# First attention of a two-layer decoder: eight heads to one context bank instead of four

## The chip, the cores and the metric

The kernel runs on one core of a Trainium2 chip. The metric is the device time of one execution in microseconds (us): the median of several runs. Beside it there is one execution recorded by the profiler, with every instruction's start and duration and every DMA packet.

Engines are named as in the profile: PE (TensorE, matrix products; PEld is its loading of weights, the stationary operand), DVE (VectorE), ACT (ScalarE), POOL (GpSimd), SP (SyncE, which issues DMAs here). A product's result lands in PSUM, which has eight banks of 128 partitions x 512 fp32; a quadrant is 32 of the partitions.

## The reference

Two layers on x of shape (8, 512, 256), each an attention and a feed-forward part, each with a residual. Only the first attention is touched by the change. With 16 heads of 16 columns, 8 batches and 512 tokens it computes

```
def _L0_attn_ref(hidden_states, attention_mask, rel_embeddings, Wq, bq, Wk, bk, Wv, bv, Wo, bo, ln_scale, ln_bias):
    ...
    scores = jnp.einsum('bhqd,bhkd->bhqk', q, k) / scale
    ...
    scores = scores + (c2p + p2c) / scale
    probs = jax.nn.softmax(scores, axis=-1)
    ctx = jnp.einsum('bhqk,bhkd->bhqd', probs, v)
    ctx = jnp.transpose(ctx, (0, 2, 1, 3)).reshape(B, S, H)
    out = ctx @ Wo + bo + hidden_states
    ...
```

c2p and p2c are scores of a query with embedded relative positions, and of a key with them. The result is normalized over its 256 columns and added to x. Everything is in fp32. After it come a feed-forward part with GELU, a second attention, and a mixture of 32 experts.

## The kernel before, in words

**Tiling.** `_l0_attention` (L90) walks over `steps` (L245): 8 batches b, 4 groups g of four heads (`NG`), 4 query tiles i of 128 tokens, 2 pairs p of heads. That makes 256 steps, 32 in a batch, 8 in a group. "Step 14" below is the step of that number within its batch; i and p follow from the number within the group (steps 0 and 1 have i = 0, steps 6 and 7 have i = 3; even steps have p = 0). The loop under `tc.manual_schedule()` (L478 to L532) is the order of the work: what a step issues goes to each engine's queue in the order written, so each engine works in order and waits at its first instruction whose data are not there.

**One step n** issues:
- `products` (L354): the scores of two heads, from `sm`, the projected queries and keys, into two PSUM banks `sc` (L363, K = 32). The pool of these banks has two, so the next step's products need the banks that DVE has read.
- `strips` (L298) for step n + 5 (`AHEAD`): position products (L306), copied by ACT (L313); a multiplication on POOL (L316); a DMA that writes them to memory in shifted rows (L323). The DMAs that read the windows `winp` and `winc` back (L332) and the two POOL additions (L343) follow one and two steps later.
- `near_keys` (L371): 4 or 6 transposes that add the windows into the score banks (L375). A step at i needs the window of i + 1, that is of step n + 2, as it landed.
- `weights` (L385): DVE adds `winc` and finds the row's extreme (L389); ACT takes the exponential and sums the row into `totals` (L391).
- `turned` (L394) for the step before: 8 PE instructions (an fp32 product is two) transpose the weights into a bank (L398), and DVE copies it out (L400).
- `weigh` (L403), on odd steps: the context of four heads for one query tile. Each head has 4 products (key tiles m) of v, 128 x 16 as weights, with `et`, 128 x 128 (L410). Head r writes rows 32 r to 32 r + 15 of the bank `ctx_ps`, one quadrant to a head, and leaves the other 16 rows of each quadrant at the zero of L237.
- one piece of side work: from `urgent`, or else from `side`, whose entries carry the step from which they may run (`later`, L252), and which is served strictly in order.

**Side work.** `project` (L275): queries and keys of the next group, two pieces at steps 0 and 1 of each group (L282). `values` (L267): v of the next batch, four pieces at steps 26 to 29 (L270, one DVE addition L273 each). `turn` and `normalized`: the next batch's normalized x, transposed. `divide`, `finish` and their parts:

When a group's last query tile is weighed (in the second step of the next group), ACT copies the bank (`c`, L421), DVE takes reciprocals of the totals (L424), and POOL spreads each of them over its head's 32 rows (`wide`, L426). `divide` (L439), queued three steps later, transposes `wide` on PE into `spread` (L442), and DVE multiplies (`cn`, L444). This happens for each of 4 groups. After the fourth group, `finish` (L447) queues four `out` (L452, one for each token tile): each sums, over the four groups' `cn`, products with `wo` (L455; `wo` has 32 rows for each head, 16 of them zero), DVE adds the result to xn (L458) and POOL adds the bias (L459). `measure` and `norm` (L461 to L469) finish the layer norm on DVE and POOL. For the last batch the four `out` are handed over as `rest` and run in `run` (L636) between the feed-forward part's first hidden products (L657).

In a batch the spreads run at steps 4 (last group of the batch before), 14, 22 and 30, and the `out` at steps 5, 6, 7 and 10.

**Start.** Outside the manual schedule, a scheduler orders the loads, the position keys (L172 to L207, with products on POOL, L203 and L206, that feed weight columns) and the clearing of eight `winc` tiles on POOL (L233).

Of the kernel before, what the change touches and what calls it, by code (L numbers as in the profile page):

```python
# [12 lines left out]
F32 = mybir.dt.float32  # L13
I32 = mybir.dt.int32
U32 = mybir.dt.uint32
AF = mybir.ActivationFunctionType
ALU = mybir.AluOpType
# [4 lines left out]
P = 128  # L22
B, S, H = 8, 512, 256
NT = S // P
NK = H // P
NH, HD = 16, 16
NG = 4
W = 256
WIN = 3 * P
NSHIFT = 4  # L30
# [59 lines left out]
def _l0_attention(nc, tc, a, x, ident, mhalf, carry, prefetch):  # L90
# [6 lines left out]
    with ExitStack() as ctx:  # L97
# [10 lines left out]
        wqk = carry.tile([P, 2, NK, NH, 32], F32, tag="w1", name="wqk")  # L108
        wq, wk = wqk[:, 0], wqk[:, 1]
        wv = wp.tile([P, NK, H], F32, tag="wv", name="wv")  # L110
        wo = carry.tile([P, NG, H], F32, tag="wo", name="wo")
        posw = carry.tile([P, 2, NG, W], F32, tag="w2", name="pos")
        posc, posp = posw[:, 0], posw[:, 1]
        bias = wp.tile([P, 4, NG], F32, tag="bias", name="bias")
# [3 lines left out]
        with tc.tile_pool(name="a_pos", bufs=1) as pp:  # L118
# [22 lines left out]
            for d in shift:  # L141
                nc.sync.dma_start(
                    d.rearrange("(q p) w -> p q w", p=P), zeros.unsqueeze(1).to_broadcast([P, 4, 2 * W])
                )
            nc.sync.dma_start(wo, a["wo_pad"].rearrange("(g p) m -> p g m", p=P))
            for name in ("bo", "ln_scale", "ln_bias"):
                nc.sync.dma_start(rows[name], a[name].partition_broadcast(P))
            for b in range(1, B):
# [76 lines left out]

        sb = pool("a_sb", 2)

        vs = [wp.tile([P, NT, H], F32, tag=f"v{n}", name=f"v{n}") for n in range(2)]

        winc = []  # L230
        for n in range(2 * NT):
# [2 lines left out]
            winc.append(w)  # L234

        ctx_ps = ps_c.tile([P, S], F32, tag="ctx", name="ctx_ps")
        nc.vector.memset(ctx_ps, 0.0)  # L237

        def near(i):

# [26 lines left out]
        def values(b, t):  # L267
            pv = misc("pv")
            for k in range(NK):
                nc.tensor.matmul(  # L270
                    pv[:, :H], xnT[:, k, t * P : (t + 1) * P], wv[:, k, :], start=k == 0, stop=k == NK - 1
                )
            nc.vector.tensor_tensor(vs[b % 2][:, t, :], pv[:, :H], rows["bv"], ALU.add)  # L273

        def project(b, g):  # L275

# [108 lines left out]
        def weights(n, j, sc):  # L385
            b, g, i, p = steps[n]
            e = sb.tile([P, S], F32, tag="e", name="e", bufs=4)
            low = sb.tile([P, 1], F32, tag="low", name="low", bufs=6)
            nc.vector.tensor_tensor_reduce(e, sc, wins[n][0][:, j, :], 1.0, -LOW, ALU.add, ALU.min, low)  # L389
            r = 2 * p + j  # L390
            nc.scalar.activation(e, e, AF.Exp, bias=low, scale=-1.0, accum_out=totals[b, g][:, i, r : r + 1])  # L391
            return e

        def turned(e):  # L394
# [8 lines left out]
        def weigh(n, ets):  # L403

            b, g, i, _ = steps[n]
            v = vs[b % 2]
            for m in range(NT):
                for r, et in enumerate(ets):
                    h = 4 * g + r
                    nc.tensor.matmul(  # L410
                        ctx_ps[32 * r : 32 * r + HD, i * P : (i + 1) * P],
                        v[:, m, HD * h : HD * h + HD],
                        et[:, m * P : (m + 1) * P],
                        start=m == 0,
                        stop=m == NT - 1,
                        skip_group_check=True,
                    )
            if i < NT - 1:
                return
            c = sb.tile([P, S], F32, tag="c", name="c", bufs=2)  # L420
            nc.scalar.copy(c, ctx_ps)  # L421

            rec = sb.tile([P, NT, 4], F32, tag="rec", name="rec")
            nc.vector.reciprocal(rec, totals.pop((b, g)))  # L424
            wide = sb.tile([P, NT, P], F32, tag="wide", name="wide", bufs=1)
            nc.gpsimd.tensor_copy(  # L426
                wide.rearrange("p i (r e) -> p i r e", e=32), rec.unsqueeze(3).to_broadcast([P, NT, 4, 32])
            )
            later(3, partial(divide, b, c, wide))
            if g == NG - 1:  # L430
                out, measure, norm = finish(b)
                if b == B - 1:
                    rest.extend([*[partial(out, t) for t in range(NT)], measure, norm])
                else:
                    later(3, *[partial(out, t, misc, sb) for t in range(NT)])
                    later(9, partial(measure, misc, sb))
                    later(12, partial(norm, misc, sb))

        def divide(b, c, wide):  # L439
            spread = ps_m.tile([P, S], F32, tag="misc", name="spread")  # L440
            for i in range(NT):
                nc.tensor.transpose(spread[:, i * P : (i + 1) * P], wide[:, i, :], ident)  # L442
            cn = carry.tile([P, S], F32, tag="cn", name="cn", bufs=5)
            nc.vector.tensor_tensor(cn, c, spread, ALU.mult)  # L444
            cns[b].append(cn)

        def finish(b):  # L447

            xn = xns[b % 2]
            stats = []  # L450

            def out(t, bank, pool):  # L452
                po = bank("po")
                for g in range(NG):
                    nc.tensor.matmul(  # L455
                        po[:, :H], cns[b][g][:, t * P : (t + 1) * P], wo[:, g, :], start=g == 0, stop=g == NG - 1
                    )
                nc.vector.tensor_tensor(xn[:, t, :], xn[:, t, :], po[:, :H], ALU.add)  # L458
                nc.gpsimd.tensor_tensor(xn[:, t, :], xn[:, t, :], rows["bo"], ALU.add)  # L459

            def measure(bank, pool):  # L461
                stats.extend(_batch_norm_stats(nc, pool, [xn[:, t, :] for t in range(NT)], 1e-7, mhalf))

            def norm(bank, pool):
                for t in range(NT):
                    _normalize(nc, xn[:, t, :], xn[:, t, :], *stats, t)
                    nc.gpsimd.tensor_tensor(xn[:, t, :], xn[:, t, :], rows["ln_scale"], ALU.mult)
                    nc.gpsimd.tensor_tensor(xn[:, t, :], xn[:, t, :], rows["ln_bias"], ALU.add)
                    nc.gpsimd.tensor_tensor(x[b][:, t, :], x[b][:, t, :], xn[:, t, :], ALU.add)  # L469

            return out, measure, norm
# [6 lines left out]
        with tc.manual_schedule():  # L478
# [7 lines left out]
            for now in range(len(steps) + 3):  # L486
                n = now
                if n < len(steps):
                    b, g, i, p = steps[n]
                    if (i, p) == (0, 0):  # L490
                        totals[b, g] = sb.tile([P, NT, 4], F32, tag="totals", name="totals", bufs=3)
                        if g in (0, NG - 1):
                            while side:
                                side.popleft()[1]()
                        if g + 1 < NG:
                            urgent.extend(project(b, g + 1))
                        elif b + 1 < B:
                            urgent.extend(project(b + 1, 0))
                            later(0, *[partial(values, b + 1, t) for t in range(NT)])
                        if g == NG - 2 and b + 1 < B:  # L500
                            measure, norm = normalized(sb, b + 1)
                            later(1, measure)
                            later(3, norm, *[partial(turn, b + 1, k) for k in range(NK)])
                    scs, parts = products(n)
                    parts.pop(0)()
                    more = parts.pop() if parts else None
                    if n + AHEAD < len(steps):
                        strips(n + AHEAD, more)
                    else:
                        if more is not None:  # L510
                            more()
                        for todo in (reads, adds):
                            if todo:
                                todo.pop(0)()
                    new = []
                    for j in range(2):
                        near_keys(n, j, scs[j])
                        new.append(weights(n, j, scs[j]))
                if n <= len(steps):
                    if es:  # L520
                        ets.extend(turned(e) for e in es)
                    es = new
                if n % 2 and len(ets) >= 4:
                    weigh(n - 3, [ets.popleft() for _ in range(4)])
                if urgent:
                    urgent.popleft()()
                elif side and side[0][0] <= n:
                    side.popleft()[1]()
                for f in prefetch.get(n - len(steps), ()):
                    f(misc, sb)  # L530
# [1073 lines left out]
    return out.reshape(*w.shape[:-1], NH * 32)  # L1604


def _experts(gate, up, down):

    first = np.concatenate([gate, up], axis=1).transpose(0, 2, 1).reshape(NE, NK, P, H).transpose(0, 2, 1, 3)
# [3 lines left out]
def _layout(v):  # L1613
# [1 line left out]
        "x": v["L0_attn_hidden_states"],  # L1615
        "wq_pad": _spread(v["L0_attn_Wq"]),
        "wk_pad": _spread(v["L0_attn_Wk"]),
        "wv": v["L0_attn_Wv"],
        "wo_pad": _spread(v["L0_attn_Wo"].T).T,
        "bq_pad": _spread(v["L0_attn_bq"]),  # L1620
        "bk_pad": _spread(v["L0_attn_bk"]),
        "bv": v["L0_attn_bv"],
        "bo": v["L0_attn_bo"],
        "ln_scale": v["L0_attn_ln_scale"],
        "ln_bias": v["L0_attn_ln_bias"],
# [35 lines left out]
```

## Time and profile before

| what | us |
| --- | --- |
| median of 3 runs | 2162.43 |
| lowest, highest run | 2162.23, 2166.1 |
| the profiled execution | 2158.92 |
| its span, first to last instruction | 2157.1 |
| first attention within it, to | about 1152 |

The profile's page gives busy time for each engine, then 40 slices of 53.9 us with the busy share in tenths. PEclk is the granted clock of TensorE in tenths of full speed. DMA is the mean busy share of 16 DMA engines. Groups of instructions are named by line and engine, with "result <- operands", shape and count, then busy time and the mean duration of one in ns, then idle time of that engine just before them. Overlapping instructions count once as busy; four products on four quadrants overlap, so their group's busy time is less than count times duration. PE durations are modelled and contain a latency, so what a stretch of PE work costs is read from its start to the start of what follows. In the order of time, a line has start, time covered, engine, line, operation, names, shapes and count, and in brackets how long the engine sat idle before and who released it.

The groups in the attention that the change is about, over the whole run: L410 has 4096 products of 274 ns and as many loads; L455 256 products of 389 ns; L442 128 of 273 ns; L421 32 copies with a median of 562 ns on ACT; L424 32 of 243 ns and L444 32 of 677 ns on DVE; L426 32 of 610 ns on POOL; L273 32 of 424 ns on DVE.

### The profile page before, as it was taken

The numbers are of one execution on the slowest core, as the hardware profiler recorded it, in microseconds if no ns is written. First come the engines' busy times: TensorE is split into PE (matmuls) and PEld (weight loads), VectorE is DVE, ScalarE is ACT, GpSimd is POOL, SyncE is SP. The second block draws the span as 40 slices with busy tenths as digits, with TensorE's granted clock in tenths as the row PEclk, the third lists the DMA queues.
The fourth block names the chain that finished last, engine by engine and source line by source line (L and its number), as shares of the span: only waits on it lengthen the run. The fifth ranks groups of instructions, "written<-read, shape, count | busy, mean of one in ns | idle before, by whom it ended". The sixth has DMA issues, their size and how long they took to land.

```text
span 2157.1 us, 46358 instructions
## 1 busy us (share of the span) xinstructions
PE 1989.8 (92%) x16100; PEld 1439.5 (67%) x16100; DVE 1401.4 (65%) x3716; ACT 1112.0 (52%) x2382; POOL 1140.5 (53%) x1342
## 2 busy tenths in 40 slices
PE   7999999999999999999998999989988877499997
PEld 4777777777777777767775666645554445388886
DVE  2576676766767677676776655337887776356666
ACT  2776666676666767667662211244444423144443
POOL 4666766767667667676673210112544544355555
PEclk7999999999999999999999999999999987699999
DMA  8998888898898988889893344900111113656888
GB/s 271 317 295 274 273 277 275 277 291 259 265 284 256 296 265 278 281 266 291 266 303 107 100 148 140 122 18 11 46 41 39 51 44 112 248 164 204 260 261 266
DMA packets 389175, 444.50 MB, mean 206 GB/s; under 512 B 43345, under 2 KB 368209, under 8 KB 388945
## 3 DMA queue, kind: packets, MB, share of 16 engines
q1 hardware_dynamic: 374160, 402.20, 61.7%
q0 software_dynamic: 13824, 38.29, 4.8%
q8 instruction: 132, 2.16, 0.4%
q10 hardware_dynamic: 960, 1.05, 0.2%
q14 instruction: 99, 0.80, 0.1%
HBM read 239.26 MB, written 202.19 MB: 205 GB/s over the span
## 4 chain that ended last, share of the span: by engine, by line
PE 27%; DVE 10%; issue 4%; POOL 4%; DMA 3%; ACT 2%; POOLq 0%; DVEq 0%; ACTq 0%; SPq 0%
PE po L665 5%; PE pge L1421 4%; PE ph L657 3%; POOL results L860 2%; PE poe L1439 2%; PE pq L916 2%; PE ao L1006 1%; DVE prod L777 1%; PE po L1035 1%; PE pv L928 1%; DVE value L777 1%; PE ps L953 1%; DVE st L52 1%; DVE xn L62 1%; PE ptr L1413 1%
## 5 line engine op out<-in xcount | busy, mean ns | idle before, releaser
L389 DVE CUSTOM_DVE_ANT_0 e<-sc,winc 128x512 f32<-128x512 f32 x512 | 333.3, 688 | 294.9 <-PE sc L375 133.6
L391 ACT ACTIVATE e<-e,low 128x512 f32<-128x512 f32 x512 | 365.9, 716 | 111.2 <-DVE low L389 105.9
L313 ACT COPY strip<-pa 128x512 f32<-128x512 f32 x512 | 275.3, 591 | 212.7 <-issue 81.3
L316 POOL TENSOR_TENSOR own<-aside,strip 128x512 f32<-128x512 f32 x256 | 268.5, 1049 | 217.5 <-ACT strip L313 198.7
L363 PE MATMUL sc<-sm,sm 32*128 32x256 f32 (+3 forms) x1792 | 323.0, 440 | 15.4 <-DVE low L389 15.4
L400 DVE COPY et<-et_ps 128x512 f32<-128x512 f32 x512 | 328.5, 683 | 0.3 <-PE et_ps L398 0.2
L306 PE MATMUL pa<-pos,sm 32*128 32x256 f32 x2048 | 301.6, 408 | 2.3 <-ACT strip L313 1.3
L398 PE MATMUL et_ps<-ident,e 128*128 128x128 f32 x2048 | 266.4, 273 | 0.2 <-DVE et L400 0.2
L860 POOL DMA_INDIRECT rows<-pay,slot x128 | 141.6, 1106 | 229.5 <-issue 216.3
L363 PEld LDWEIGHTS sc<-sm,sm 32*128 32x128 f32 x1792 | 162.3, 184 | 124.6 <-issue 49.6
L398 PEld LDWEIGHTS et_ps<-ident,e 128*128 128x128 f32 x2048 | 232.6, 142 | 0.6 <-ACT e L391 0.5
L343 POOL TENSOR_TENSOR winp<-winp,own 128x256 f32<-128x256 f32 x256 | 186.5, 728 | 74.8 <-DMA winp<-shift 63.7
L860 POOL DMA_INDIRECT results<-y,r x160 | 155.8, 974 | 122.1 <-ACT y L1441 74.7
L375 PE MATMUL sc<-ident,winp 128*128 128x128 f32 x1280 | 199.7, 285 | 5.3 <-DMA winp<-shift 5.0
L343 POOL TENSOR_TENSOR winc<-winc,own 128x256 f32<-128x256 f32 x256 | 186.6, 729 | 34.1 <-DMA winc<-shift 31.0
L306 PEld LDWEIGHTS pa<-pos,sm 32*128 32x128 f32 x2048 | 180.9, 188 | 15.0 <-ACT strip L313 4.7
L375 PEld LDWEIGHTS sc<-ident,winp 128*128 128x128 f32 x1280 | 136.3, 141 | 81.4 <-issue 63.2
L57 POOL TENSOR_TENSOR rstd<-var,mhalf 128x4 f32<-128x4 f32 x40 | 44.8, 1121 | 252.6 <-DVE var L55 230.6
L1421 PE MATMUL pge<-store,rT 128*128 x640 | 167.9, 385 | 1.1 <-DVE rT L1415 0.5
L410 PE MATMUL ctx_ps<-et,v 128*16 128x128 f32 x4096 | 137.2, 274 | 0.2 <-DVE et L400 0.2
L660 ACT ACTIVATE hT<-ph,b 128x512 f32<-128x512 f32 x64 | 44.0, 687 | 169.8 <-PE ph L657 169.8
L282 PE MATMUL pq<-xnT,wqk 128*128 128x512 f32 x256 | 126.1, 614 | 3.6 <-DVE xnT L77 3.6
(216 smaller groups left out, 3421.4 us busy)
## 6 DMA issues: line engine op xcount, KB each, us to landing
shift<-strip SPq DMA_DIRECT2D x256, 510.0 KB
winp<-shift SPq DMA_DIRECT2D x128, 384.0 KB
winc<-shift SPq DMA_DIRECT2D x128, 384.0 KB
winp<-shift SPq DMA_DIRECT2D x128, 256.0 KB
winc<-shift SPq DMA_DIRECT2D x128, 256.0 KB
rows<-empty SPq DMA_DIRECT2D x8, 2640.0 KB
r<-rows SPq DMA_DIRECT2D x160, 132.0 KB
z<-results SPq DMA_DIRECT2D x32, 512.0 KB
```

The source lines that it names most:

```text
L306: nc.tensor.matmul(pa[:, t * W : (t + 1) * W], src[rs, i * P : (i + 1) * P], pos[rs, g, :], start=True, stop=True)
L313: nc.scalar.copy(st[:, 2 * j : 2 * j + 2, :].rearrange("p t w -> p (t w)"), pas[j])
L316: nc.gpsimd.tensor_tensor(own, aside.unsqueeze(2).to_broadcast([P, 2, 2, P]), st[:, :, W - 1 : W].rearrange("p (j t) o -> p t j o", t=2).t ...
L343: nc.gpsimd.tensor_tensor(dst, dst, own[:, t], ALU.add)
L363: nc.tensor.matmul(sc[:, c0:c1], s[side_][rs, cut : cut + P], s[2 + side_][rs, c0:c1], start=c0 == 0, stop=False, skip_group_check=True,)
L375: nc.tensor.matmul(sc[:, m * P : (m + 1) * P], wins[n + 2 * (m - i)][1][:, j, (i - m + 1) * P : (i - m + 2) * P], ident, start=False, stop ...
L389: nc.vector.tensor_tensor_reduce(e, sc, wins[n][0][:, j, :], 1.0, -LOW, ALU.add, ALU.min, low)
L391: nc.scalar.activation(e, e, AF.Exp, bias=low, scale=-1.0, accum_out=totals[b, g][:, i, r : r + 1])
L398: nc.tensor.transpose(et_ps[:, ms], e[:, ms], ident)
L400: nc.vector.tensor_copy(et, et_ps)
L860: ins = nc.gpsimd.indirect_dma_start(to, bass.IndirectOffsetOnAxis(ap=index, axis=0), source, None, bounds_check=last)
L1421: nc.tensor.matmul(pg[:, :H], rT[:, k * P : (k + 1) * P], w[:, k * H : (k + 1) * H], start=k == 0, stop=k == NK - 1)
```

## The change

Two groups, 2 k and 2 k + 1, share the context bank. In each quadrant the even group's head has the first 16 rows and the odd group's the last 16. For this, v is kept as 32 columns for each head, 16 of them zero: in the first half for heads of even groups, in the second for heads of odd ones, so that a product of 32 columns adds zeros to the other head's rows. The two halves of v are cleared once, on POOL, and written by two DVE additions for each token tile. Only the first product on each quadrant, of the even group at i = 0, starts a new sum in the bank. `wv` and `bv` come with their columns in the order even groups, odd groups. `totals` holds eight heads. The copy of the bank, the reciprocals, `wide` and `divide` run once for two groups, after the odd one; `out` sums over two `cn` instead of four, and `wo` has 256 rows without zeros. The number of context products, 16 for each weigh (32 PE instructions), stays. In a batch, the spreads of steps 14 and 30 no longer occur.

```diff
+NC = NG // 2
@@
-        wo = carry.tile([P, NG, H], F32, tag="wo", name="wo")
+        wo = carry.tile([P, NC, H], F32, tag="wo", name="wo")
@@
-            nc.sync.dma_start(wo, a["wo_pad"].rearrange("(g p) m -> p g m", p=P))
+            nc.sync.dma_start(wo, a["wo_rows"].rearrange("(g p) m -> p g m", p=P))
@@
-        vs = [wp.tile([P, NT, H], F32, tag=f"v{n}", name=f"v{n}") for n in range(2)]
+        vs = [wp.tile([P, NT, 2, NH // 2, 2 * HD], F32, tag=f"v{n}", name=f"v{n}") for n in range(2)]
+        for v in vs:
+            nc.gpsimd.memset(v, 0.0)
@@
-        nc.vector.memset(ctx_ps, 0.0)
@@
-            nc.vector.tensor_tensor(vs[b % 2][:, t, :], pv[:, :H], rows["bv"], ALU.add)
+            by_head = lambda w: w.rearrange("p (h d) -> p h d", d=HD)
+            for o in range(2):
+                s = slice(o * H // 2, (o + 1) * H // 2)
+                nc.vector.tensor_tensor(
+                    vs[b % 2][:, t, o, :, HD * o : HD * o + HD], by_head(pv[:, s]), by_head(rows["bv"][:, s]), ALU.add
+                )
@@
-            nc.scalar.activation(e, e, AF.Exp, bias=low, scale=-1.0, accum_out=totals[b, g][:, i, r : r + 1])
+            r = 2 * r + g % 2
+            nc.scalar.activation(e, e, AF.Exp, bias=low, scale=-1.0, accum_out=totals[b, g // 2][:, i, r : r + 1])
@@
-                        ctx_ps[32 * r : 32 * r + HD, i * P : (i + 1) * P],
-                        v[:, m, HD * h : HD * h + HD],
+                        ctx_ps[32 * r : 32 * r + 32, i * P : (i + 1) * P],
+                        vs[b % 2][:, m, g % 2, g // 2 * 4 + r, :],
                         et[:, m * P : (m + 1) * P],
-                        start=m == 0,
-                        stop=m == NT - 1,
+                        start=m == 0 and i == 0 and not odd,
+                        stop=m == NT - 1 and odd,
@@
-            if i < NT - 1:
+            if i < NT - 1 or not odd:
                 return
@@
-            rec = sb.tile([P, NT, 4], F32, tag="rec", name="rec")
-            nc.vector.reciprocal(rec, totals.pop((b, g)))
+            rec = sb.tile([P, NT, 8], F32, tag="rec", name="rec")
+            nc.vector.reciprocal(rec, totals.pop((b, g // 2)))
@@
-                wide.rearrange("p i (r e) -> p i r e", e=32), rec.unsqueeze(3).to_broadcast([P, NT, 4, 32])
+                wide.rearrange("p i (r e) -> p i r e", e=HD), rec.unsqueeze(3).to_broadcast([P, NT, 8, HD])
@@
-                for g in range(NG):
+                for g in range(NC):
                     nc.tensor.matmul(
-                        po[:, :H], cns[b][g][:, t * P : (t + 1) * P], wo[:, g, :], start=g == 0, stop=g == NG - 1
+                        po[:, :H], cns[b][g][:, t * P : (t + 1) * P], wo[:, g, :], start=g == 0, stop=g == NC - 1
                     )
@@
-        "wv": v["L0_attn_Wv"],
-        "wo_pad": _spread(v["L0_attn_Wo"].T).T,
+        "wv": _odd_last(v["L0_attn_Wv"]),
+        "wo_rows": v["L0_attn_Wo"].reshape(NC, 2, 4, HD, H).transpose(0, 2, 1, 3, 4).reshape(H, H),
```

## The prediction

> **What bounds the kernel now.** I read the page first, then stretches of the first attention, the groups by line and shape, and the order of time inside single steps.
>
> ```profile
> span 2157.1 us, 46358 instructions
> PE 1989.8 (92%) x16100; PEld 1439.5 (67%) x16100; DVE 1401.4 (65%) x3716; ACT 1112.0 (52%) x2382; POOL 1140.5 (53%) x1342
> PE   7999999999999999999998999989988877499997
> PEclk7999999999999999999999999999999987699999
> DMA  8998888898898988889893344900111113656888
> ```
>
> The change lies in slices 1 to 21 (the first attention, to about 1152 us). TensorE is at nine tenths there with its full clock, and the DMA engines are at eight to nine tenths: two candidates. A stretch of about one batch (32 steps; the same spread starts at 248.70 and again at 386.26, so 137.6 us), columns length, PE, PEld, DVE, ACT, POOL, clock, DMA share, GB/s:
>
> ```profile
> 200.00:340.00 140.00, 136.59 (x1567) 102.72 (x1565) 98.78 (x241) 95.94 (x218) 96.09 (x121) 1.00 0.89 278
> ```
>
> PE is busy for 97.6%. DVE, ACT and POOL have 30% to spare; DMA has 11%. What PE waits for shows inside it: I took each stretch of equal matmuls and the time to the next stretch, and compared it with the shortest of its kind. Of the 1092 us from 60 to 1152, 78 are above those shortest times; most recur in each batch where a score bank is released late by VectorE (0.47 to 0.61 us in a step in which PE has nothing beside it), not by a DMA. So PE's own work is some 93% of this stage, and work taken out shortens it wherever no such wait takes its place.
>
> **Projection.** `out` issues for each token tile 4 fp32 products over K=128, as 8 PE instructions (two passes); the change leaves 2 products, 4 instructions. What an `out` of 4 costs is in the profile already: `values` has the same form (128*128, 128x256, x4), in the same place of a step and with one VectorE add behind it. Two answers in order of time, an `out` and a `values`, both behind the context products:
>
> ```profile
> 346.17 1.99 PE L455 MATMUL po<-wo,cn 128*128 128x256 f32 x8
> 348.09 0.59 PE L363 MATMUL sc<-sm,sm 32*128 32x384 f32 x2
> ```
>
> ```profile
> 443.24 1.13 PE L270 MATMUL pv<-wv,xnT 128*128 128x256 f32 x4
> 444.31 0.48 PE L363 MATMUL sc<-sm,sm 32*128 32x256 f32 x2
> ```
>
> From start to next start: 348.09 - 346.17 = 1.92 us against 444.31 - 443.24 = 1.07; the difference, 0.86, is four instructions at 0.215 (256 rows, two passes). 28 outs run in the attention (7 batches x 4): 28 x 0.86 = 24.1 us. The last batch's 4 run between the first hidden products of the FFN, where PE runs without a gap from 1160 to 1184: another 4 x 0.86 = 3.4. Does the shorter step stay PE-bound? The steps with `values` take 3.62 and 4.81 us (even, odd), against 4.48 and 5.68 with `out`: they keep the difference, under the same VectorE load. Projection: -27.5 us.
>
> **Softmax division.** It goes from 32 to 16 runs. Removed 16 times: ACT's copy c (0.562 us), DVE's product cn (0.677), POOL's wide (0.610), 4 PE transposes; 32 reciprocals of 0.243 become 16 of 128x32 (estimate 0.26, from 16 more elements in each). That is 9.0 us of ACT, 14.4 of DVE and 9.8 of POOL, none of them the bound. On PE a spread is worth little, since it fills a wait:
>
> ```profile
> 386.26 0.60 PE L442 MATMUL spread<-ident,wide 128*128 128x128 f32 x4
> 387.62 1.20 PE L363 MATMUL sc<-sm,sm 32*128 32x384 f32 x3 [0.76 <-DVE low L389]
> ```
>
> ```profile
> 455.18 0.60 PE L442 MATMUL spread<-ident,wide 128*128 128x128 f32 x4
> 455.71 0.74 PE L363 MATMUL sc<-sm,sm 32*128 32x384 f32 x2
> ```
>
> In each batch four spreads run, at steps 4, 14, 22 and 30. The changed schedule drops those of steps 14 and 30 (groups 0 and 2). The first of these two rows is step 14: the score products wait 0.76 us longer for VectorE, which normalizes the batch before it. Without the spread they wait until the same moment: gain 0. The second is step 30 (3.12 us). Without the spread PE's own work is 0.49 + 0.97 + 1.08 = 2.53, but a step with nothing beside it waits about 0.47 us for VectorE: 3.00. Gain 0.12 x 8 = 1.0 us. The bounds: 0, and, if all waits went too, 16 x 0.44 + 8 x 0.83 = 13.6 us (a spread is worth 0.87 + 0.53 - 0.97 = 0.44 on a PE without waits). I take 1.0, which the two rows support.
>
> **Context products, now 32 columns wide.** Their number stays 4096, but each loads 128x32 weights instead of 128x16, half of them zeros.
>
> ```profile
> L410 PEld LDWEIGHTS ctx_ps<-et,v x4096: 92/97/97, 71.9 to 1151.4; 128*16 128x16 f32 x196
> ```
>
> ```profile
> L953 PEld LDWEIGHTS ps<-prod,heads x192: 106/109/178, 1431.7 to 1785.3; 128*32 128x32 f32 x192
> ```
>
> The wide load takes 12 ns more. Where does it land? The products run as rounds of four, one for each quadrant; the rounds start 109 ns apart (in one weigh at 606.913, 607.022, 607.131 us), which is also the spacing of the L398 transposes (8 in 0.87 us), whose 128-column loads take 142 ns. A load eight times as wide thus hides behind a stream of 128 rows, and so will this. Only the first round of a weigh has nothing to hide behind: 128 x 0.012 = 1.5 us. Here a rule speaks against the change: the Trainium skill, "TensorE: Matmul & The Clock Gate", Part 3 (The mechanism, "What overlaps and what doesn't") lets a weight load overlap running matmuls only if the row groups differ. All these loads use all rows. By the rule every load is exposed, 4096 x 0.012 = 49 us more; by the row 1.5. If it held, the L398 stream couldn't keep 109 ns a piece; I take the row, and keep the rule as a rival.
>
> **The rest.** `values` writes v in two VectorE adds of 128x128: 2 x 0.288 (the row of L1427, same size, from a bank) for 0.424, so 0.15 us in each of 32 places; VectorE is idle 0.78 us before the next score in such a step. Cost 0; 32 x 0.15 = 4.9 if that cover is gone, and not below 0. The totals' column stride changes no count. PE accumulates even and odd groups in one bank, so the only wait for its copy now comes after two groups: gain 0 to 1. At the start POOL clears two v of 128x2048 (twice a winc memset of 0.95 each, 3.6 us pipelined) ahead of the weight products L203; today three winc memsets and 1.53 us of idle time stand there (4.25 us), so it fits. The winc memsets move behind, some 4 us later, to about 30 us; the first window read goes out at 45. Cost 0, at most 3. On SP the order is the same; wo's load halves (256 KB less, about 0.9 us at 274 GB/s), and nobody waits for it then: 0. VectorE's memset of the context bank ran while it waited for x: 0.
>
> **DMA.** The steps shorten by 3.4 us a batch and the DMA work stays: share 0.89 x 137.6 / 134.1 (137.6 - 4 x 0.86) = 0.91, while 60 to 200 us ran at 0.95. Counting packets by size in a batch, a window read lands about 4 us after issue and is used 1 to 4.7 us later. The reads whose two steps contain outs have 2.1 to 4.3, and lose at most 1.7. I book 1 us given back; between 0 and, if half of the projection's gain in the attention goes into waits, 12.
>
> **Sum** against the profiled execution (2158.92 us; 2157.1 and 1.8 around the span): -27.5 - 1.0 + 1.5 + 1.0 = -26.0, so 2132.9. The median of the runs before, 2162.43, lies 3.5 above that execution; I carry the difference over: 2136.4, given as 2136.
>
> **Rivals.**
> 1. Waits for windows take over (up to 12 us more than booked): 2137 to 2149. For: 0.91 to 0.95 is near the highest share seen, and DVE e waited 31.6 us in all for winp. Against: PE waited 5 us for windows in the whole stage, and the spare times above. 0.13.
> 2. The removed division takes its waits along: 2136 less up to 12.6, so 2124. For: the 0.83 wait behind the spread recurs in most batches. Against: VectorE's normalization causes it and stays. 0.09.
> 3. Slower: loads in the context products are exposed, 12 ns in each. 2136 + 47.5 = 2184. It decides from 26 us on, which is 6.5 ns a load. Against: 109 ns a round leaves nothing exposed today. 0.03.
> 4. It does not do what it says, that is, outs don't shorten their steps, since VectorE or the windows set them: about 2162. Against: `values` steps. 0.03.
> Forecast: 2129 to 2143, 0.72.
>
> The range for 8 in 10 is 2126 to 2148: all of the forecast, most of rival 1, part of 2. A difference under 0.2% (4.3 us) can't be told from none. Faster 0.94 (forecast, 1, 2), same 0.03 (4), slower 0.03 (3).
>
> **What would show it.** Right: `po` with 128 PE instructions, 1.06 us to the next score products behind context products; even and odd steps with an out near 3.6 and 4.8; rounds of context products still 109 ns apart with loads of about 109 ns; a batch of 134 us; step 30 at 3.0 and step 14 unchanged. Wrong: rounds at 120 ns or more (rival 3); PE `sc` L375's successor waiting for `winp` in steps 5 to 12, with a DMA share at 0.95 (rival 1); step 14 shorter by 0.8 (rival 2). The second attention and the experts should not move; if they do, the cause is not in this sum.

## The result, and the profile after

| | before | changed |
| --- | --- | --- |
| median of 4 runs, us | 2162.73 | 2134.41 |
| lowest, highest, us | 2162.23, 2166.1 | 2132.01, 2136.61 |
| the profiled execution, us | 2158.92 | 2132.52 |
| one batch (32 steps, median of batches 1 to 6), us | 137.5 | 134.4 |

The ratio is 0.9862 with a 95% interval of 0.9846 to 0.9879. The predicted 2136 is 1.6 us above the median, and inside the runs.

The page of the changed kernel, with the rows that answer to those shown of before:

```profile
span 2130.7 us, 46004 instructions
PE 1963.5 (92%) x15908; PEld 1415.5 (66%) x15908; DVE 1393.8 (65%) x3715; ACT 1104.7 (52%) x2366; POOL 1138.3 (53%) x1328
PEclk7999999999999999999999999999999987699999
DMA  8998989898898989989883544900111114556788
```

PE lost 192 instructions (128 of the outs, 64 of the spreads), 26.3 us of its busy time and 26.4 us of the span: work on the engine that is the bound came out, and its share of the span stayed at 92%. The same stretch of 140 us as before, same columns:

```profile
200.00:340.00 140.00, 136.80 (x1581) 102.54 (x1580) 100.44 (x248) 98.02 (x223) 98.30 (x123) 1.00 0.92 286
```

PE is as busy as it was (136.80 us against 136.59), but more steps fit: DVE, ACT and POOL do more in it, and the DMA share is 0.92 instead of 0.89. Two steps with an `out`, PE in order of time; the first is behind context products, as the two rows in the prediction were:

```profile
476.88 1.13 PE L463 MATMUL po<-wo,cn 128*128 128x256 f32 x4
477.94 0.59 PE L371 MATMUL sc<-sm,sm 32*128 32x384 f32 x2
...
480.38 1.03 PE L463 MATMUL po<-wo,cn 128*128 128x256 f32 x4
481.34 0.59 PE L371 MATMUL sc<-sm,sm 32*128 32x384 f32 x2
```

477.94 - 476.88 = 1.06 us to the next score products, where it was 1.92. Measured from one step's near-key products (L383) to the next's, the four steps of a batch with an `out` went from 5.68, 4.27, 5.46 and 4.48 us to 4.83, 3.40, 4.61 and 3.62: 0.85 to 0.87 each. Steps 14 and 30, which lost their spread, stayed as they were (4.40 and 4.39 us, 3.12 and 3.12). The context products, by their own row (min/median/max in ns):

```profile
L418 PEld LDWEIGHTS ctx_ps<-et,v x4096: 106/110/178, 70.8 to 1123.8; 128*32 128x32 f32 x196
```

The load of 32 columns takes 13 ns more than that of 16 (median 97 before). From the second on, the rounds of four that it belongs to still start 109 ns apart; only the time from the first to the second round of a weigh grew, from 0.120 us (606.793 to 606.913 before) to 0.134 (610.097 to 610.231 now).

### The profile page after: what moved, and what is told of

It is laid out like the page before. It is cut to its first block, busy times and chain, and to the rows that moved or that the text cites. A ratio compares the mean times of both kernels' runs of the same rounds, so it can differ in the third digit from the quotient of the medians.

```text
span 2130.7 us, 46004 instructions
## 1 busy us (share of the span) xinstructions
PE 1963.5 (92%) x15908; PEld 1415.5 (66%) x15908; DVE 1393.8 (65%) x3715; ACT 1104.7 (52%) x2366; POOL 1138.3 (53%) x1328
## 4 chain that ended last, share of the span: by engine, by line
PE 32%; DVE 10%; issue 4%; ACT 2%; SPq 1%; DMA 1%; POOL 1%; POOLq 0%; DVEq 0%; ACTq 0%
PE pge L1430 7%; PE po L674 5%; PE poe L1448 3%; PE ph L666 3%; PE pq L925 2%; PE ao L1015 2%; PE ptr L1422 2%; DVE prod L786 1%; PE pv L937 1%; DVE value L786 1%; PE po L1044 1%; SPq L1387 1%; PE ps L962 1%; DVE st L53 1%; DVE xn L63 1%
## 5 line engine op out<-in xcount | busy, mean ns | idle before, releaser
L351 POOL TENSOR_TENSOR winp<-winp,own 128x256 f32<-128x256 f32 x256 | 186.9, 730 | 76.8 <-DMA winp<-shift 63.0
L383 PE MATMUL sc<-ident,winp 128*128 128x128 f32 x1280 | 199.6, 285 | 5.8 <-DMA winp<-shift 5.8
L383 PEld LDWEIGHTS sc<-ident,winp 128*128 128x128 f32 x1280 | 136.4, 141 | 80.7 <-issue 59.6
L418 PE MATMUL ctx_ps<-et,v 128*32 128x128 f32 x4096 | 140.0, 277 | 0.2 <-DVE et L409 0.2
```

The costliest lines, as they stand in the source:

```text
L351: nc.gpsimd.tensor_tensor(dst, dst, own[:, t], ALU.add)
L383: nc.tensor.matmul(sc[:, m * P : (m + 1) * P], wins[n + 2 * (m - i)][1][:, j, (i - m + 1) * P : (i - m + 2) * P], ident, start=False, stop ...
```

## The experiments

The medians of the kernel before were 2166.05, 2172.2 and 2177.49 us on the three chips used here, so ratios to it are compared, not times. The expectations are in the times of the first chip; a ratio times 2162.73 puts a result on that scale. "Changed" is the kernel after the change. Lines of the edits that are left out are marked "...".

**e1: the projection's two products put back.** `wo` of the changed kernel gets two more slabs, cleared to zero on POOL, and each `out` four products again; the sums stay the same.

```diff
-        wo = carry.tile([P, NC, H], F32, tag="wo", name="wo")
+        wo = carry.tile([P, NG, H], F32, tag="wo", name="wo")
...
+            nc.gpsimd.memset(wo[:, NC:, :], 0.0)
...
-                for g in range(NC):
+                for g in range(NG):
...
-                        po[:, :H], cns[b][g][:, t * P : (t + 1) * P], wo[:, g, :], start=g == 0, stop=g == NC - 1
+                        po[:, :H], cns[b][g % NC][:, t * P : (t + 1) * P], wo[:, g, :], start=g == 0, stop=g == NG - 1
```

> The changed kernel, but each out issues 8 PE instructions again: two more products, with a wo of zeros, are summed into the same bank. Nothing else moves; the division stays at 16 runs. Theory (the gain is the projection's PE time): 28 outs in the attention and 4 in the FFN get 0.86 us back each, +27.5: about 2162 us (2157 to 2166), with steps 5, 6, 7 and 10 at 5.69, 4.26, 5.46 and 4.48 us again. Rival (the halved division carries a part of the gain): the time stays well below the kernel before, 2140 to 2152.

Measured: 2161.19 us, ratio 0.998 (0.997 to 0.999). PE in order of time, in step 6 of the batch shown above:

```profile
489.21 1.89 PE L464 MATMUL po<-wo,cn 128*128 128x256 f32 x8
491.03 0.59 PE L372 MATMUL sc<-sm,sm 32*128 32x384 f32 x2
```

1.82 us to the next score products, against 0.96 in the changed kernel. The four steps are back at 5.69, 4.27, 5.47 and 4.48 us and a batch at 137.5. With the projection's products back, 0.2% (0.1 to 0.3) is left of the change's 1.4%: the gain is the projection. What the 0.2% is stays open; no step of the attention accounts for it.

**e2: the division put back.** After each even group the changed kernel also copies the bank, takes reciprocals, spreads and multiplies; the result is not used.

```diff
-            if i < NT - 1 or not odd:
+            if i < NT - 1:
                 return
+            if not odd:
+                ...
+                nc.scalar.copy(c, ctx_ps)
+                ...
+                nc.vector.reciprocal(rec, totals[b, g // 2][:, :, 0::2])
+                ...
+                later(3, partial(divide, b, c, wide, False))
```

> The changed kernel, with a division after each even group as well (copy of the bank, reciprocals, wide, 4 transposes, multiplication), at its old places in steps 14 and 30; its result is not used. Theory (the spreads of steps 14 and 30 only fill waits for VectorE): steps 14 and 30 stay at 4.39 and 3.12 us, total 2134 to 2138. Rival (the division takes its waits along): 0.44 to 1.3 us for each of 16, so 2141 to 2155.

Measured: 2140.34 us, ratio 0.9878 (0.9861 to 0.9895), on the scale of the first chip 2136.3, as the theory had it; the interval overlaps that of the changed kernel. The steps decide: 14 and 30 take 4.38 and 3.12 us with the spread and 4.39 and 3.12 without, and batches 1 to 6 take 805.1 us together against 806.6 in the changed kernel. PE in step 30 of a batch, first in this kernel, then in the changed one:

```profile
581.98 1.04 PE L407 MATMUL et_ps<-ident,e 128*128 128x128 f32 x8
582.86 0.60 PE L461 MATMUL spread<-ident,wide 128*128 128x128 f32 x4
583.38 0.74 PE L371 MATMUL sc<-sm,sm 32*128 32x384 f32 x2
...
584.61 0.66 PE L383 MATMUL sc<-ident,winp 128*128 128x128 f32 x4
```

```profile
581.77 1.04 PE L407 MATMUL et_ps<-ident,e 128*128 128x128 f32 x8
582.74 1.17 PE L371 MATMUL sc<-sm,sm 32*128 32x384 f32 x3
...
584.40 0.66 PE L383 MATMUL sc<-ident,winp 128*128 128x128 f32 x4
```

Counted from the start of the transposes, the score products begin 1.40 us later with the spread (583.38 - 581.98) and 0.97 without. From there to the next near keys it is 1.23 us with it and 1.66 without: the sum is 2.63 in both. The first score bank is free early, but the second is released at the same moment as ever: VectorE ends its pass over it 1.50 us after the start of the transposes in both kernels (at 583.48 and 583.27). No bracket shows this wait, because the products of the two heads are interleaved with each other and with the position products, and some PE instruction is always in flight. The floor of such a step in these traces is 3.12 us.

**e3: the wide loads alone.** The kernel before gets loads of 32 columns: its head's and the following one's, whose sums land in the unused rows of the quadrant, where zero rows of `wo` meet them.

```diff
-        vs = [wp.tile([P, NT, H], F32, tag=f"v{n}", name=f"v{n}") for n in range(2)]
+        vs = [wp.tile([P, NT, H + HD], F32, tag=f"v{n}", name=f"v{n}") for n in range(2)]
...
-                        ctx_ps[32 * r : 32 * r + HD, i * P : (i + 1) * P],
-                        v[:, m, HD * h : HD * h + HD],
+                        ctx_ps[32 * r : 32 * r + 32, i * P : (i + 1) * P],
+                        v[:, m, HD * h : HD * h + 32],
```

> The kernel before, but each context product loads 32 columns of v: those of the head and of the one after it, so the other 16 rows of a quadrant receive that head's sums instead of staying zero; wo has zeros for them. Everything else is as before. Theory (loads hide behind the stream, only the start of a weigh sees them): 128 x 0.014 = 1.8 us, so 2163 to 2166, rounds of four still 109 ns apart. Rival (the rule that loads of the same row group do not overlap with products): 4096 x 0.012 = 49 us, so about 2211.

Measured: 2168.57 us, ratio 1.0009 (1.0 to 1.0018). Its 4096 loads take what they take in the changed kernel:

```profile
L412 PEld LDWEIGHTS ctx_ps<-et,v x4096: 106/110/178, 71.3 to 1153.2; 128*32 128x32 f32 x196
```

Steps with a weigh are 0.014 us longer, all others unchanged; 128 x 0.014 = 1.8 us, 0.08%. Loads that all ran in the open would have cost 49 us, 2.3%: rival 3, and the rule behind it (the Trainium skill, "TensorE: Matmul & The Clock Gate", Part 3, "What overlaps and what doesn't"), do not hold for this stream. The same Part, ahead of that rule, also lets a load go ahead if it targets a background weight buffer; these rows would fit that, but no run here shows where a load goes.

**e5: one product for an `out`.** What would a further halving give? This kernel leaves out the heads of two of the four groups, so it serves for its time alone.

```diff
-                for g in range(NC):
+                for g in range(1):
-                        po[:, :H], cns[b][g][:, t * P : (t + 1) * P], wo[:, g, :], start=g == 0, stop=g == NC - 1
+                        po[:, :H], cns[b][g][:, t * P : (t + 1) * P], wo[:, g, :], start=True, stop=True
```

> The changed kernel, but each out sums only the first of its two cn (2 PE instructions): the projection leaves out the heads of groups 2 and 3. A third point beside 8 and 4 instructions. Theory (PE sets the steps): 0.43 us less in each out unless the step then waits for VectorE, about 1.6 a batch, so -11 in the attention and -1.7 in the FFN: 2119 to 2125. Rival (window DMAs or VectorE set the steps from here on): 2130 to 2134.

Measured: 2128.46 us, ratio 0.9819 (0.9804 to 0.9833): 0.43%, or 9.3 us, below the changed kernel's ratio. On the scale of the first chip that is 2123.6 us, inside the range of the theory, though the sum in it had 12.7. The four steps fell by 0.44, 0.28, 0.43 and 0.39 us instead of 0.43 each. Step 6 stopped at 3.12 us, the floor found above; its score products show the same stretched form:

```profile
477.30 0.60 PE L463 MATMUL po<-wo,cn 128*128 128x256 f32 x2
477.83 0.74 PE L371 MATMUL sc<-sm,sm 32*128 32x384 f32 x2
...
479.06 0.66 PE L383 MATMUL sc<-ident,winp 128*128 128x128 f32 x4
```

1.54 x 7 = 10.8 us were to be had in the attention. In the profiled executions it is 10.2 us shorter than in the changed kernel, from the first to the last near-key products; TensorE's clock, of which below, fell three times in e5 and took some of it. From the first to the last hidden product the feed-forward part is only 0.4 us shorter (222.2 us against 222.6): behind the shorter outs its transposes wait 0.67 us for VectorE's `xn`. So in step 6 another engine does take over, 0.28 us below what the change reached; the odd steps are still PE's.

**a2: the changed kernel again**, on another chip.

> The changed kernel itself, for comparison with the next two on the same chip: ratio 0.986 to the kernel before. Its profile shows whether the second attention and the experts take other times in another execution of the same program (theory: they do, by some us; rival: the change shifted them, and they take the same again).

Measured: 2142.08 us, ratio 0.9845 (0.9826 to 0.9864). Same program, a span of 2142.8 us instead of 2130.7: the medians of the attention's steps are the same, but for steps 1 and 25 with late windows (5.68 and 5.59 us instead of 5.46), while from the last hidden products to the second attention's first projection it takes 22.3 us instead of 17.3, and from there to its last projection 295.1 instead of 290.7. Those stages vary by some us between chips or executions with nothing changed.

**e4: side work where PE waits anyway, first try.** PE's waits for VectorE recur in even steps; odd ones have the context products. So the changed kernel's side pieces are held back to even steps, except for those without PE work.

```diff
-                elif side and side[0][0] <= n:
+                elif side and side[0][0] <= n and (n % 2 == 0 or side[0][1] in light):
...
```

> The changed kernel, but side work with PE instructions (divide, out, turn, values) is served on even steps only, in the same order; what is not served by then runs before steps 24 and 0, as now. Theory (PE has nothing beside it in a bare even step and waits 0.4 to 0.5 us for VectorE there, and none in an odd step): a piece costs 0.39 instead of 1.06 us where it moves to an even step; five pieces a batch move, some are bunched before steps 0 and 24: about -2 us a batch, 2118 to 2127. Rival (window DMAs set the pace): no gain, 2130 or more.

A miss: 2163.91 us, ratio 0.995 (0.9933 to 0.9968), slower than the changed kernel. The moved pieces did become cheaper (steps 5 and 7: 3.77 and 3.55 us instead of 4.83 and 4.61). But the queue is served strictly in order, so the measuring and the normalization behind the held pieces came together, one after the other, late in a group. In the batch shown VectorE measures in step 19; POOL, still at the output's normalization of the batch before, delivers the standard deviations (`rstd`) only at 550.8. VectorE in step 21 of a batch, and PE's stops from 60 to 1050 us (who waits, for whom; us in total, times, longest):

```profile
550.83 3.71 DVE L63 TENSOR_SCALAR xn<-x,mv,rstd 128x256 f32<-128x256 f32 x4 [3.27 <-POOL rstd L58]
554.46 0.68 DVE L397 CUSTOM_DVE_ANT_0 e<-sc,winc 128x512 f32<-128x512 f32 x1
```

```profile
PE sc L371 <- DVE low L397: 39.9, 20, 5.0
```

VectorE stands for 3.27 us until POOL has the standard deviations, works 3.71 us on four tiles, and only then touches the scores; PE stops for 4.96 us, and its granted clock is at half from 552.3 to 559.1. The step takes 10.3 us (median of the batches). The rival's range, 2130 or more, came true without its cause: windows stop PE for only 4.1 us in all.

**e6: second try, with two queues.** PE's pieces run on even steps only, in an order that keeps one to a step. Measuring and normalizing go to a queue of their own on odd steps, the normalization one tile at a time and far behind the measuring; `xn` gets a third buffer, `cn` two instead of three. The main lines:

```diff
+        def prepare(b, n):
+            measure, norm = normalized(sb, b)
+            light.append((n, measure))
+            light.extend((n + 2, partial(norm, (t,))) for t in range(NT))
...
-                    later(9, partial(measure, misc, sb))
-                    later(12, partial(norm, misc, sb))
+                    light.append((now + 14, partial(measure, misc, sb)))
+                    light.extend((now + 18, partial(norm, misc, sb, (t,))) for t in range(NT))
...
-                elif side and side[0][0] <= n:
+                elif n % 2 and light and light[0][0] <= n:
+                    light.popleft()[1]()
+                elif n % 2 == 0 and side and side[0][0] <= n:
```

> The changed kernel with all its side work spread: pieces with PE instructions on even steps only, one each (values 26, 28, 30, 2; divide 4, 22; out 6, 10, 12, 14; turn 18, 20), measuring and normalizing cut to one tile a piece and put on odd steps; normalized x has three buffers instead of two, cn two instead of three. Theory (PE's own work and VectorE's short waits set the steps): even steps 3.1 to 3.6 us, odd 3.55 to 3.77, with projections 4.25 and 5.46: about 124.5 us a batch instead of 134.4, so 2060 to 2075. Rival (the DMA engines are the bound at 122 us of work a batch; no stretch was above a share of 0.95): 128 us a batch or more, 2088 to 2105.

Measured: 2091.76 us, ratio 0.9624 (0.9603 to 0.9644); beside the changed kernel on the same chip that is another 50.3 us less. On the scale of the first chip it is 2081.4, between the ranges of theory and rival, so the theory promised too much. A batch takes 126.3 us, halfway between the 124.5 of PE's own work and the 128 of the rival. One batch, the columns as in the stretches above:

```profile
433.80:559.84 126.04, 125.34 (x1493) 95.37 (x1489) 94.68 (x236) 93.41 (x211) 92.66 (x117) 1.00 0.96 301
```

PE is busy for 99.4%, and the DMA engines for 96%. One step stuck out: 30, with 4.36 us instead of 3.40. VectorE, in order of time, in the step before it and in it:

```profile
551.39 0.42 DVE L53 BATCH_NORM_STATS2 st<-x 128x6 f32<-128x256 f32 x1
...
553.64 0.17 DVE L56 TENSOR_SCALAR var<-mv 128x4 f32<-128x4 f32 x1
553.85 0.69 DVE L402 CUSTOM_DVE_ANT_0 e<-sc,winc 128x512 f32<-128x512 f32 x1
```

From 551.39 to 553.81 VectorE measures four tiles in a row; the scores of step 30, whose near keys began at 551.93, wait for it. How much of the rest of the shortfall is due to the DMA engines, at 96% of their time, no run here separates; windows stop PE for 5.3 us between 60 and 1050 us.

**e7: the measuring in two halves**, with e6 beside it. The helper that measures one half is not shown.

```diff
-            light.append((n, measure))
+            light.extend((n, partial(measure, s)) for s in range(2))
...
-                    light.append((now + 14, partial(measure, misc, sb)))
+                    light.extend((now + 12 + 2 * s, partial(measure, misc, sb, s)) for s in range(2))
```

> The kernel of e6_spread_side with the measuring of four tiles (mean and variance on VectorE, one run of about 2.4 us) cut into two pieces of two tiles each, at two odd steps; everything that is computed stays. In e6 step 30 takes 4.36 us instead of 3.40 in six batches: VectorE is at its measuring until 553.85 in one of them and touches the next scores only then, and PE waits for the score bank. Step 16 shows the same in small (4.40 instead of 4.25). Theory (the long VectorE run is the cause): step 30 at 3.40, step 16 at 4.25, 6 x 0.96 + 7 x 0.15 = 6.8 us less than e6, a ratio of 0.9968 to e6. Rival (a window that lands late, since the DMA engines are at 0.96 of their time, or the order of PE's own work): step 30 stays at 4.36 and the time is that of e6 within 2 us.

> The kernel of e6_spread_side once more, beside e7_split_measure on the same chip. Expected: a ratio to the kernel before of 0.960 to 0.965, a batch of 126.3 us and step 30 at 4.36 us, as in its first run. If its time differs by over 0.3% in ratio, the difference of the two schedules cannot be read from their ratios, only from their steps.

Measured: e6 2092.86 us, ratio 0.9619 (0.9606 to 0.9633), step 30 at 4.36 again. With two halves 2084.51 us, ratio 0.9567 (0.9554 to 0.958): 0.9960 of e6, where the theory said 0.9968. Step 30 takes 3.40 us in every batch but the last, where nothing is left to measure, and step 16 4.25 in six of eight. Batches 1 to 6 take 750.7 us together, against 757.0 and 758.8 in the two profiles of e6. The whole profiled executions do not show the gain: that of e7 is the slowest of its five (2092.07 us), with late windows and a clock at half in its last batch. PE's stops from 60 to 1050 us, before, changed, and in this version:

```profile
PE sc L363 <- DVE low L389: 13.8, 24, 0.9
PE pt L264 <- DVE xn L62: 4.6, 8, 0.8
PE sc L375 <- DMA winp<-shift: 2.1, 6, 0.6
```

```profile
PE sc L371 <- DVE low L397: 18.1, 27, 1.2
PE pt L267 <- DVE xn L63: 4.0, 7, 0.6
PE sc L383 <- DMA winp<-shift: 3.5, 7, 1.1
```

```profile
PE sc L406 <- DMA winp<-shift: 8.1, 10, 1.9
PE pt L647 <- DVE xn L81: 0.8, 2, 0.4
PE sc L394 <- DVE low L420: 0.3, 1, 0.3
```

The stops for VectorE are all but gone, and what is left are windows that land late, most of them at steps 1, 24 and 25. This version beats both kernels: 3.0% below the changed one by their ratios, taken on two chips (0.9567 / 0.9862 = 0.970). What it would give without the eight-head banks was not tried.

## Why the prediction was right, step by step

| term | predicted, us | measured, us |
| --- | --- | --- |
| projection, attention | -24.1 | 28 outs at -0.86: -24.1 |
| projection, feed-forward | -3.4 | -3.8 (226.4 to 222.6 from first to last hidden product) |
| division, step 14 | 0 | 0 (4.40 to 4.39) |
| division, step 30 | -1.0 | 0 (3.12 to 3.12) |
| wide loads | +1.5 | 128 x 0.014: +1.8 |
| windows | +1.0 | +1.4 (PE's stops, 2.1 to 3.5), within the scatter |
| sum of these terms | -26.0 | -24.7 |
| profiled execution | -26.0 | -26.4 |

**Projection.** Right to the second digit in the attention, because its price was read from a row of the same form in the same place (`values`), and because the same kind of step showed that the shorter step is still PE's. e1 shows that it is the cause. In the feed-forward part it gave 0.4 more: the first of the four `out` runs while TensorE's clock is low (2.79 us for its 8 instructions before, 1.56 for 4 now, -1.23), the other three give 0.87 each.

**Division.** The mis-sized term, if a small one: 1.0 us booked, none seen. The prediction gave step 30 a wait of 0.47 us, taken from steps with nothing beside them, and so 3.00. The second score bank keeps it at 3.12, with the spread (e2) or without, and e5's step 6 ran into the same floor. The argument itself, that a spread fills a wait, held, and rival 2 (12.6 us) got nothing. Step 14 is its plainest case: without the spread PE waits for the same VectorE pass, and the bracket is 0.41 us longer (1.17 against the 0.76 behind the spread in the prediction), near the 0.44 that the prediction counts for a spread:

```profile
380.32 1.20 PE L371 MATMUL sc<-sm,sm 32*128 32x384 f32 x3 [1.17 <-DVE low L397]
```

**Loads.** Right in kind and nearly in size; e3 is the direct test. Only the first round of a weigh pays.

**Windows.** Nothing that can be told from none. PE's stops for windows were 2.1, 2.3 and 1.8 us in before, e3 and e1, 3.5 and 3.4 in the two profiles of the changed kernel, but 4.4 in e2 and 0.9 in e5, whose steps are shorter still. Nor are they where the prediction looked: steps 5 to 12 lost nothing beyond 0.13 us once, and the longest stop is at step 24. So rival 1, windows taking over, did not come. e6 and e7 bear the same transfers at a share of 0.96 to 0.97 and lose 5 to 9 us by them, so they were not near to taking over at 0.91 to 0.92.

**What the sum did not hold.** That the total agrees to 0.4 us is partly luck: the measured terms add up to 24.7 us, and the rest is a balance of events that no term has. At the last near-key products the changed kernel is 27.7 us ahead, after the feed-forward part about 32, at the end 26.4: the later stages took 5 us more, which the prediction said should not move. The stretch from the second attention's last projection to the experts' first products took 183.0 us before and 186.9 in the changed kernel; but e3, which is the kernel before but for the loads, took 186.8 there, on another chip. So the profiled execution of before was short in this stretch, and the change need not be the cause. In the attention single events of some us (a window that landed late in before's last batch, a fall of the clock in its batch 3) went the change's way, and its first near-key products came 1.2 us earlier.

## What to carry to other kernels

Price removed work by a row of the same form in the same place of the schedule, and ask of the same row whether the shorter step still belongs to the same engine; here that gave the 0.86 us of each `out`. Work of the bounding engine cost next to nothing in a step in which it waited for another, and its full price elsewhere, so where the pieces were put was worth more than halving one of them: 28 us by the change, 50 us by moving pieces without removing any. When moving them, keep long runs of a second engine (four tiles measured or normalized at once) away from the step whose score it must release, since PE stops until that run is over.

## What the runs showed that was not expected

**A short stop can cost more than its own length.** Step 14's stop of 1.17 us leaves PE busy for 1.83 of 3 us, and now and then its clock falls just behind it. The changed kernel in stretches of 3 us (columns as above; the granted clock is third from the end):

```profile
376.00:379.00 3.00, 3.00 (x52) 2.55 (x43) 3.00 (x6) 1.87 (x5) 2.69 (x5) 1.00 0.93 272
379.00:382.00 3.00, 1.83 (x18) 1.21 (x16) 3.00 (x7) 1.52 (x4) 2.77 (x5) 1.00 0.83 258
382.00:385.00 3.00, 3.00 (x23) 2.65 (x24) 2.30 (x7) 2.57 (x6) 2.84 (x5) 0.54 1.00 325
385.00:388.00 3.00, 3.00 (x52) 2.37 (x42) 0.55 (x2) 0.02 (x1) 2.84 (x4) 0.89 1.04 292
```

(0.46 + 0.11) x 3 us is 1.7 us of clock lost, so 3.4 us at half clock; from 382.23 to 385.64 the trace's own record has a granted clock of 0.50. That is the length of one window that the Trainium skill, "TensorE: Matmul & The Clock Gate", Part 1, gives. Step 15 took 5.16 us instead of 3.55, and step 16 won 0.7 back, since it then waited less. The page has the clock fall after an idle window; here PE was busy for 2.24 of the 3.41 us before the fall. That share alone does not bring it about: from 511.93 to 515.35 PE is busy for 2.25 us, around the same stop in the next batch, and no fall follows.

The stop recurs in batches 1 to 7. Behind it the clock fell twice in the changed kernel (batches 2 and 7), twice when that ran again and three times in e5, so in 7 of 21 batches; not once in the 28 of before, e1, e2 and e3. e6 and e7 have no such stop. Without the spread at step 14 PE stands longer there (1.17 us instead of 0.76), which may make a fall likelier; but e1 lacks that spread too and shows no fall, and so few events do not settle it. In e4 the clock was at half for some 44 us in all up to 1020 us, around its long stops.

**A wait without a bracket.** With two heads' products interleaved on PE, a late second bank shows only as a longer stretch (1.66 us to the next near keys, where step 30 in e6 takes 551.93 - 550.86 = 1.07), not as idle time. PE's stops from 60 to 1050 us add up to 26 us in the changed kernel, while moving its pieces saved 50.
